# One column of softmax weights brought into row 0 of the masked weights by two transfers through DRAM instead of a ninth transposition

## The chip, the core and the metric

The kernel runs on one core of a Trainium2 chip. The time is that of the whole program on the device, in microseconds (us): the median of several runs. A core has a matrix engine (PE, whose weight loads are listed apart as PEld), a vector engine (DVE), a scalar engine (ACT), a general engine (POOL), and a sequencer (SP) that issues the DMA transfers here. Each of them works through its own instructions strictly in the order in which the program lists them and waits for the others through semaphores. Operands lie in SBUF (128 partitions); PE writes to PSUM, which has 8 banks here; the inputs, the output and some intermediate tiles lie in DRAM. A DMA is issued by SP and is carried by 16 DMA engines, as packets.

## The reference

The input x is (2, 4096, 256). First comes one recurrent attention stage (an RWKV scan with a group norm and an output projection, added to x), then a layer norm and two layers of local attention and a gated feed-forward part. Everything is float32. The change lies in the local attention, which has 8 heads of 64, in windows of 128 tokens that see their own window and the one behind:

```python
bq = q.reshape(b, h, w, WINDOW, d) * QK_SCALE
bk, bv = (look_around(bk), look_around(bv))      # window behind, own window: 256 keys
sim = jnp.einsum('bhwid,bhwjd->bhwij', bq, bk)
i = bt[:, :, None]
j = btk[:, None, :]
mask = (i < j) | (i > j + WINDOW) | (j == -1)
sim = jnp.where(mask, -jnp.finfo(sim.dtype).max, sim)
attn = jax.nn.softmax(sim, axis=-1)
out = jnp.einsum('bhwij,bhwjd->bhwid', attn, bv)
```

Query number i of a window sees its own keys 0 to i, and of the window behind the keys i to 127. That makes 129 keys for each query, and the last key behind, number 127, is seen by every query.

## The kernel before

**Steps.** The two layers of both sequences are 32 blocks of 512 tokens; each block has four windows, so the attention is 128 steps n, one window each. Four of them are the first window of a sequence in a layer ("lone": no window behind). The other 124 steps do what is told here. The first 64 steps are the two layers of the first sequence. Its recurrence comes before them; that of the second sequence runs as filler between the first 55 steps or so, and the feed-forward matmuls of an earlier block fill the rest of each step (`fill`).

**129 columns in place of 256.** `scores` (line 1086) makes, for a pair of heads, a bank of 256 columns: the keys behind, then the own keys. `softmax` (line 1110) takes the columns from 127 on: column 0 is the last key behind, columns 1 to 128 are the own keys. Where an own key k is after the query, and so masked, `copy_predicated` first writes the score of key k-1 behind into its place, since just those are visible. So tile `pr` (128 queries x 8 heads x 129) holds all the visible weights without a gap; ACT makes the exponentials, and ACT or DVE scales each head by its reciprocal sum (the groups `pr<-pr,sums`, ACT line 520 and DVE line 518). Column 0 is also added to column 1 beforehand.

**Two products.** `values` (line 1183) computes the output of a step, transposed, as own values times all 128 weights, plus a correction: `dv` holds, in row k, value k-1 behind minus own value k (row 0: value 127 behind minus own value 0), and `pB` holds the same weights where they belong to a key behind, zero elsewhere, with row 0 the weights of the last key behind. `pB` is 128 keys x 8 heads x 128 queries.

**`transpose_p`** (line 1157) is called twice per step, for four heads each time (s = 0 and 1). PE transposes the four 128x128 blocks of `pr` into a bank; ACT or DVE copies the bank to `pT`, and DVE multiplies it by the mask `backs` into `pB`. With s = 1 comes the part that the change replaces: the 8 columns number 0 (128 queries x 8 heads) are transposed by PE into 8 rows of a bank, copied to the tile `last` by ACT or DVE, and sent by one DMA from these 8 partitions to row 0 of `pB`. `pB` has one buffer, `last` two, `pr` two.

**Where `pB` is needed.** The matmuls of `values(n)` stand in one piece with `scores(n + 1)`, behind the 16 matmuls of the scores; the correction matmuls (`bank<-pB,dv`) read all rows of `pB`, row 0 too.

**What sets the order.** The kernel does not issue its instructions directly. `Plan.note` records each operation with its reads and writes; `Plan.cost` (line 302) gives it a duration; `Plan.order` (line 376) then plays the engines forward. Each engine takes next the operation that can start first, and among those the one with the earlier due row (`plan.at(n)`). Consecutive matmuls into one bank are a piece and stay together. Copies marked `either` go to ACT, or to DVE when ACT is busy for more than 700 ns longer. `Plan.give` (line 508) writes the result down; that is why nearly every instruction carries its line, 524 (`scaled` on ACT: 520, on DVE: 518). A DMA is entered with a landing time and the time that it occupies the queue:

```python
o.passes = size / 170 if ways == 16 else size / (25 * ways)
inner = len(views) == 2 and not any(v.place.outer for v in views)
o.step = 370 if not inner else 580 if ways in (1, 16) else 800
o.time = LAND + o.passes
```

with `LAND = 2500` (ns). All DMAs are issued by SP, in one planned order. Between the steps' other work SP issues, for each step, `vr<-vt` (three DMAs: the values behind moved down by a row, read by POOL for `dv`), `h<-x` (four: the shift before the feed-forward part), a table `tab`, the row of `pB`, and in every second step `kT<-kT`.

Of the kernel before, what the change touches and what calls it, by code (L numbers as in the profile page):

```python
# [9 lines left out]
F32 = mybir.dt.float32  # L10
# [5 lines left out]
P = 128  # L16
B, S, D = 2, 4096, 256
HD_A = 16
L, HEADS, DH, W = 2, 8, 64, 128
# [41 lines left out]
LEAN = 700  # L61
SLACK = 1.06
LOAD = 1283
LAND = 2500
TURN = {"row": 195, "col": 95, "full": 199}
SETS = {AF.Exp: 1, AF.Tanh: 1, AF.Gelu: 2, AF.Ln: 3}
# [15 lines left out]
class View:  # L82
# [51 lines left out]
    def to_broadcast(self, shape):  # L134
        return View(
            self.place,
            self.rows,
            np.broadcast_to(self.idx, shape[1:]),
            [*self.chain, ("to_broadcast", (shape,), {})],
        )  # L140

    def bitcast(self, dtype):
        return View(self.place, self.rows, self.idx, [*self.chain, ("bitcast", (dtype,), {})])
# [37 lines left out]
class Plan:  # L181
# [35 lines left out]
    def bank(self, shape):  # L217

        return self.view(Place(T, True), 0, shape)

    def dram(self, shape, name):
        place = Place(int(np.prod(shape[1:])))
        place.outer = True
        place.real = self.dram_pool.tile([P, place.size], F32, tag=name, name=name)
        return self.view(place, 0, shape)

    def at(self, row):
# [74 lines left out]
    def cost(self, o):  # L302

        views = [*o.outs, *o.ins]
# [4 lines left out]
        if o.eng == "tensor":  # L309
            trans = name == "transpose"  # L310
            left = o.args[1]
            move = o.args[2] if len(o.args) > 2 else o.args[1]
            cols = max(move.idx.size, left.idx.size) if not trans else P
            o.step = (1 if trans else 2) * (cols / 1.2 + (2 if cols >= 256 else 3))
            if not trans and left.shape[0] <= 64:
                o.half = "row"
            elif not trans and left.idx.size <= 64:
                o.half = "col"
            if o.half != "full":
                o.step /= 2  # L320
            o.time = o.step + 150
        elif o.eng == "vector":
            d = 150 + 1.04 * n
            if name == "tensor_tensor_reduce":
                d = 240 + 1.04 * n
            elif name == "tensor_tensor_scan":
                d, o.lock = 203 + 2.1 * n, True
            elif name == "scalar_tensor_tensor":
                d, o.lock = 200 + 1.05 * n, inside > 1
            elif name == "tensor_tensor":  # L330
                o.lock = inside > 1
            elif name == "tensor_scalar":
                d, o.lock = 155 + (1.27 if psum else 0.98) * n, not psum and n > 16
            elif name == "tensor_copy" and not psum:
                d, o.lock = 230 + 0.45 * n, n > 16
            elif name == "bn_aggr":
                d = 172
            elif name == "reciprocal":
                d = 147 + 4 * n
            o.step, o.time = max(d - 85, 60), d  # L340
        elif o.eng in ("scalar", "either"):
            d = (160 if psum else 195) + 0.83 * n
            if name == "scaled":
                d = 305 + 0.76 * n
            elif name == "activation":
                o.set = SETS.get(o.args[2])
                if o.args[2] == AF.Identity:
                    d = 365 + 0.87 * n
                elif isinstance(o.kw.get("bias"), View):
                    d += 85  # L350
            o.step, o.time = d - 100, d
            if "accum_out" in o.kw:
                o.time = d + 200
        elif o.eng == "gpsimd":
            o.lock = name != "memset"
            if name == "tensor_tensor":
                d = 430 + 156 * n if ALU.pow in o.args else 140 + 2.22 * n
            elif name == "tensor_scalar":
                d = 230 + 1.12 * n
            else:  # L360
                d = (100 if name == "memset" else 187) + 0.98 * n
            o.step, o.time = d, d
            hold = d if n > 64 else 100
        else:
            v = min(views, key=lambda v: v.shape[0] * v.idx.size)
            size = 4 * v.shape[0] * v.idx.size
            rows = max(v.shape[0] if v.shape[0] > 1 else v.shape[1] for v in views)
            ways = max(k for k in range(1, 17) if rows % k == 0)
            o.passes = size / 170 if ways == 16 else size / (25 * ways)
            inner = len(views) == 2 and not any(v.place.outer for v in views)  # L370
            o.step = 370 if not inner else 580 if ways in (1, 16) else 800
            o.time = LAND + o.passes
# [155 lines left out]
def kernel(ctx: ExitStack, tc: tile.TileContext, a: dict, out: bass.AP):  # L528
# [581 lines left out]
    def softmax(n, g):  # L1110
# [42 lines left out]
        for m in range(2):  # L1153
            ph = prs[n][:, h0 + 2 * m, off:]
            nc.either.scaled(ph, ph, sums[:, m : m + 1])

    def transpose_p(n, s):


# [14 lines left out]
            ALU.mult,  # L1174
        )
        if s:
            pt = bank([P, W])
            nc.tensor.transpose(pt[:HEADS, :], pr[:, :, 0], ident)
            last = tile_of([P, W], "last", 2)[:HEADS]
            either(last, pt[:HEADS, :])  # L1180
            nc.sync.dma_start(out=pBs[n][0:1], in_=last)

    def values(n):

# [187 lines left out]
    for b, parts in enumerate(ARENA):  # L1372
        o = 0
# [231 lines left out]
```

## Time and profile before

| | |
|---|---|
| median of 3 runs | 2972.16 us (2969.49 to 2972.76) |
| the profiled execution, its own time | 2970.99 us |
| its span (first to last instruction) | 2969.2 us |
| PE busy | 2945.0 us, 99% |
| weight loads (PEld) | 1913.7 us, 64% |
| DVE, ACT, POOL busy | 76%, 68%, 49% |
| DMA engines | 20.9% on the queue of SP's transfers |
| TensorE clock granted | 0.998 |
| transpositions of the four-head blocks, `mats,pr 128*128` | 1024 |
| transpositions of column 0, `mats,pr 128*8` | 124, 33.8 us busy |
| copies of them to `last` | 97 on ACT (24.2 us), 27 on DVE (7.3 us) |
| DMA issues `pB<-last` | 124, 0.69 us each on SP |

In rows of groups the name before `<-` is the tile that is written, behind it those that are read; `128*8 128x128` means weights of 128x8 and 128 columns streamed. A matmul's listed duration holds its way through the pipeline, so matmuls overlap: how long one holds PE up is read from the distance between starts. An `[idle before <-X]` behind a row of the timeline tells how long the engine was idle before it and whose work ended that. For SP the timeline lists the time that it spends on issuing a DMA, not the transfer itself. The trace also has every DMA packet with its size, start and duration, and the updates of the semaphores, from which the landing of a transfer follows.

### The profile page before, as it was taken

The page shows a single profiled execution, that of the slowest core. Times are in us where ns is not written, and L with a number is a line of the kernel's source. Part 1 is how long each engine was busy: PE and PEld are TensorE (multiplying, and loading weights), DVE is VectorE, ACT ScalarE, POOL GpSimd, SP SyncE. Part 2 cuts the span into 40 slices and gives each one's busy share as a digit, 9 for nine tenths or more (in the row PEclk, how much of TensorE's full clock was granted, in tenths as well). Part 3 has the DMA queues.
Part 4 walks back from the last instruction along what each step waited for, and adds up shares of the span by engine and source line. Part 5 has one row for each costly group of instructions (what it writes and reads, how often), then busy time and mean ns, then how long its engine had stood idle before and what let it go on. Part 6 is the DMA issues. An engine that isn't in the chain of part 4 may idle for free.

```text
span 2969.2 us, 48964 instructions
## 1 busy us (share of the span) xinstructions
PE 2945.0 (99%) x15548; PEld 1913.7 (64%) x15548; DVE 2250.9 (76%) x5088; ACT 2018.8 (68%) x5359; POOL 1449.3 (49%) x1705
## 2 busy tenths in 40 slices
PE   9999999999999999999999999999999999999998
PEld 4476766666666666666666666666666666666665
DVE  7889999998866788786777677777676676767673
ACT  7887787778666777776666666666666666666663
POOL 2226654555554555445555444545454554555550
PEclk9999999999999999999999999999999999999999
DMA  2324322221121211111122221111112211111110
GB/s 85 114 78 133 115 69 87 75 82 53 60 65 54 83 48 53 56 59 55 52 77 79 74 68 48 61 58 61 55 44 70 70 57 49 58 55 54 47 40 27
DMA packets 185227, 195.09 MB, mean 66 GB/s; under 512 B 27812, under 2 KB 148484, under 8 KB 184456
## 3 DMA queue, kind: packets, MB, share of 16 engines
q1 hardware_dynamic: 184968, 191.96, 20.9%
q8 instruction: 123, 2.02, 0.3%
q14 instruction: 136, 1.11, 0.1%
HBM read 85.46 MB, written 39.85 MB: 42 GB/s over the span
## 4 chain that ended last, share of the span: by engine, by line
PE 92%; DVE 3%; ACT 3%; issue 1%; POOL 0%; DMA 0%; SPq 0%; POOLq 0%; ACTq 0%; DVEq 0%
PE bank L524 92%; ACT pr L524 1%; ACT L524 1%; DVE arena L524 1%; DVE bank L524 0%; ACT pr L520 0%; DVE sq L524 0%; DVE qk L524 0%; DVE h L524 0%; DVE nmx L524 0%; DVE hm L524 0%; DVE pB L524 0%; ACT arena L524 0%; ACT oT L524 0%; ACT hm L524 0%
## 5 line engine op out<-in xcount | busy, mean ns | idle before, releaser
L524 PE MATMUL bank<-wqkv,xT 128*128 128x512 f32 x1536 | 723.8, 596 | 0.5 <-ACT xT L524 0.5
L524 PE MATMUL bank<-hT,w 128*128 128x512 f32 (+1 forms) x1408 | 652.2, 595 | 0.0
L524 POOL TENSOR_TENSOR t<-qk,tab 128x256 f32<-128x256 f32 x512 | 383.6, 768 | 471.2 <-ACT qk L524 362.3
L524 ACT ACTIVATE pr<-bank,nmx 128x129 f32<-128x129 f32 (+1 forms) x1024 | 369.5, 379 | 147.8 <-DVE nmx L524 146.4
L524 PEld LDWEIGHTS bank<-hT,w 128*128 128x128 f32 (+1 forms) x1408 | 254.8, 189 | 260.9 <-issue 247.3
L524 PEld LDWEIGHTS bank<-wqkv,xT 128*128 128x128 f32 x1536 | 266.4, 191 | 210.9 <-issue 207.3
L524 POOL TENSOR_TENSOR rn<-rn,mhalf 128x16 f32<-128x16 f32 x128 | 391.7, 3060 | 8.8
L520 ACT ACTIVATE pr<-pr,sums 128x129 f32<-128x129 f32 (+1 forms) x948 | 334.1, 418 | 40.7 <-DVE pr L524 39.9
L524 DVE COPY_PREDICATED bank<-packs,bank 128x254 f32<-128x254 int32 x496 | 186.4, 420 | 229.8 <-PE bank L524 229.7
L524 PE MATMUL bank<-w,hm 128*128 128x256 f32 x1280 | 294.0, 381 | 0.0
L524 POOL TENSOR_TENSOR dv<-vr,vt 128x512 f32<-128x512 f32 x124 | 165.4, 1334 | 201.2 <-PE bank L524 188.1
L524 PEld LDWEIGHTS bank<-w,hm 128*128 128x128 f32 x1280 | 239.7, 190 | 35.0 <-issue 4.2
L524 ACT COPY qk<-bank 128x512 f32<-128x512 f32 x225 | 132.3, 588 | 170.5 <-PE bank L524 164.0
L524 PE MATMUL bank<-kT,qT 64*128 64x256 f32 (+1 forms) x2048 | 246.1, 380 | 0.4 <-ACT kT L524 0.4
L524 PE MATMUL bank<-wo,oT 128*128 128x256 f32 x1024 | 243.0, 380 | 1.4 <-ACT oT L524 1.3
L524 PEld LDWEIGHTS bank<-wo,oT 128*128 128x128 f32 x1024 | 193.4, 190 | 70.5 <-ACT oT L524 22.6
L524 PEld LDWEIGHTS bank<-kT,qT 64*128 64x128 f32 x2048 | 190.4, 187 | 68.8 <-issue 36.0
L524 DVE TENSOR_TENSOR pB<-bank,backs 128x512 f32<-128x512 f32 x248 | 170.0, 686 | 83.5 <-PE bank L524 56.7
L524 ACT ACTIVATION_READ_ACCUMULATOR pr<-bank,nmx 128x1 f32 x1024 | 221.8, 217 | 0.0
L524 ACT COPY hm<-bank 128x512 f32<-128x512 f32 x170 | 99.8, 587 | 174.1 <-PE bank L524 173.1
L524 PEld LDWEIGHTS bank<-mats,pr 128*128 128x128 f32 x1148 | 134.9, 135 | 115.7 <-issue 73.2
L524 PE MATMUL bank<-pT,vt 128*64 128x128 f32 x2048 | 203.3, 279 | 0.0
(159 smaller groups left out, 5625.3 us busy)
## 6 DMA issues: line engine op xcount, KB each, us to landing
vr<-vt SPq DMA_DIRECT2D x124, 224.0 KB
tab<-in_c_rot_dram SPq DMA_DIRECT2D x128, 128.0 KB
kT<-kT SPq DMA_DIRECT2D x64, 256.0 KB
z<-zd SPq DMA_DIRECT2D x16, 512.0 KB
x<-in_x_dram SPq DMA_DIRECT2D x16, 512.0 KB
x1d<-x SPq DMA_DIRECT2D x16, 512.0 KB
x<-x1d SPq DMA_DIRECT2D x16, 512.0 KB
h<-x SPq DMA_DIRECT2D x128, 64.0 KB
```

What stands on the lines that cost most here:

```text
L520: self.nc.scalar.activation(dst, src, AF.Copy, scale=scale)
L524: getattr(getattr(self.nc, o.eng), name)(*args, **kw)
```

## The change

In the second call of `transpose_p` of each of the 124 steps the transposition, its bank, the copy and the DMA from `last` go. In their place SP issues two DMAs. The first reads column 0 of the 8 heads from `pr` (128 partitions, 8 values of 4 bytes in each, 516 bytes apart) and writes each value to its place in a row of 1024 in a DRAM tile `front` (two of these, used in turn): value of query q and head h to place 128 h + q. The second copies that row of 4 KB to row 0 of `pB`. In the built program the first is a transfer of 128x8x1 and the second one of 1x1024; the second waits for the landing of the first. The planner is told a duration for it: where neighbours in a view aren't one element apart, the queue is taken to be occupied for `SINGLES`, 1500 ns. The whole program is planned anew with these costs.

```diff
+SINGLES = 1500
 LAND = 2500
...
+    def seen(self, pattern, **sizes):
+
+        return View(self.place, self.rows, self.idx, [*self.chain, ("rearrange", (pattern,), sizes)])
...
-        place.real = self.dram_pool.tile([P, place.size], F32, tag=name, name=name)
+        place.real = self.dram_pool.tile([shape[0], place.size], F32, tag=name, name=name)
...
             o.passes = size / 170 if ways == 16 else size / (25 * ways)
+            if any(v.idx.size > 1 and v.idx.ravel()[1] != v.idx.ravel()[0] + 1 for v in views):
+                o.passes = SINGLES
...
+    fronts = [plan.dram([1, HEADS * W], f"front_{i}") for i in range(2)]
+
     def transpose_p(n, s):
...
         if s:
-            pt = bank([P, W])
-            nc.tensor.transpose(pt[:HEADS, :], pr[:, :, 0], ident)
-            last = tile_of([P, W], "last", 2)[:HEADS]
-            either(last, pt[:HEADS, :])
-            nc.sync.dma_start(out=pBs[n][0:1], in_=last)
+            row = fronts[n % 2]
+            nc.sync.dma_start(out=row.seen("o (h q) -> (o q) h", h=HEADS), in_=pr[:, :, 0])
+            nc.sync.dma_start(out=pBs[n][0:1].rearrange("o h q -> o (h q)"), in_=row)
```

## The prediction

> **What bounds the kernel now.** I read the page first, then the chain of waits over a long stretch, then one step in the timeline. The page's busy shares and its chain:
>
> ```profile
> span 2969.2 us, 48964 instructions
> ...
> PE 2945.0 (99%) x15548; PEld 1913.7 (64%) x15548; DVE 2250.9 (76%) x5088; ACT 2018.8 (68%) x5359; POOL 1449.3 (49%) x1705
> ...
> PE 92%; DVE 3%; ACT 3%; issue 1%; POOL 0%; DMA 0%; SPq 0%; POOLq 0%; ACTq 0%; DVEq 0%
> ```
>
> A busy PE need not be PE at its pace, so the chain between 1515 and 2177 us (columns: start, duration, what):
>
> ```profile
> 1 pieces in order of time: start us, us, what
> 1514.98 662.03 PE bank L524 x3611
> ```
>
> For 662 us, some 31 steps, one matmul follows the other and nothing else is on the chain. In the records of the matmuls a 128x512 matmul starts 429 ns after its like, 128x256 after 216, a 128x128 transposition after 109, nearly everywhere. The sum over the span leaves 24.2 us with PE idle (2969.2 - 2945.0). So PE's own work sets the time; what is taken from PE is won, what is added elsewhere is free as long as PE doesn't wait for it.
>
> The step around 1510 us (start, duration, instruction):
>
> ```profile
> 1506.89 0.60 PE L524 MATMUL bank<-mats,pr 128*128 128x128 f32 x4
> ...
> 1508.33 1.46 SPq L524 DMA_DIRECT2D vr<-vt  x2
> ...
> 1508.42 0.69 ACT L520 ACTIVATE pr<-pr,sums 128x129 f32<-128x129 f32 x2 [0.31 <-DVE pr L524]
> ...
> 1509.83 0.83 SPq L524 DMA_DIRECT2D h<-x  x1
> ...
> 1510.76 0.71 PE L524 MATMUL bank<-mats,pr 128*128 128x128 f32 x5
> ...
> 1511.88 0.25 ACT L524 COPY last<-bank 8x128 f32<-8x128 f32 x1
> ...
> 1512.69 0.68 DVE L524 TENSOR_TENSOR pB<-bank,backs 128x512 f32<-128x512 f32 x1
> ...
> 1513.46 0.73 SPq L524 DMA_DIRECT2D pB<-last  x1
> ...
> 1522.07 0.39 PE L524 MATMUL bank<-pB,dv 128*64 128x128 f32 x4
> ```
>
> The weights are complete at 1509.1, the row goes out only at 1513.46, when DVE's masking has ended (row 0 is written by both), and the first reader of pB runs at 1522.07. I took these times for all 124 steps. Counted from the complete weights, masking ends after 1.7 to 13.4 us (median 4.7); pB's first reader starts after 5.8 at the least (the last step), under 8 in 4 steps, under 9 in 13, median 13.1. The old DMA's semaphore is full 1.81 us after its issue starts; from there 1.6 to 10.2 us pass until the reader, median 5.2.
>
> **What is removed.** 124 transpositions. The five of 1510.76 take 0.71 us where the four of 1506.89 take 0.60; in the records the instruction after the eight-column one starts 109 ns later (median): 124 x 0.109 = 13.5 us, on the path, as PE is saturated. Its weight load (87 ns) lies beside the matmul before. The copies (97 on ACT, 24.2 us, and 27 on DVE, 7.3 us) lie beside PE on engines busy for 68 and 76%: nothing. One bank less is in use for about 1 us a step: between nothing and the 8.1 us that weight loads wait for DVE's work in banks (they run beside matmuls): nothing.
>
> **What is added, and its cover.** (a) SP issues one DMA more per step: 0.33 (128x1024, SBUF to DRAM) to 0.70 us (kT, 4x128 pieces); I take 0.7 for the shape with several dimensions: 124 x 0.7 = 87 us on a queue whose 1544 issues last 915 us together. Hidden. (b) The column transfer, from issue to landing; call it F. It moves 1024 pieces of 4 bytes, 64 per DMA engine, and no such piece to DRAM is in this trace. The nearest row is kT's transfer, alone in this window of 3.04 us:
>
> ```profile
> DMA packets 544, 0.27 MB, mean 88 GB/s; under 512 B 24, under 2 KB 544, under 8 KB 544
> ...
> q1 hardware_dynamic: 544, 0.27, 31.0%
> ```
>
> 0.310 x 16 x 3.04 us / 544 = 27.7 ns a packet; it lands 2.7 us after issue, against 1.8 for the 8 pieces of the old row: 32 packets per engine cost 0.9 us, back to back. Lowest end: 9 ns, the duration of the 4-byte semaphore writes, F = 1.75 + 64 x 0.009 = 2.3. Highest: 189 ns, the mean of the 4 KB packets, F = 13.8. Between: 53.7 ns, the mean over all packets of the queue (20.9% x 16 x 2969.2 / 184968), F = 5.1. I take kT's 27.7, as it too is many small pieces: F = 1.75 + 1.77 = 3.5. (c) The second transfer lands as the table's does (128 KB out of DRAM, 2.05 us after issue), 0.24 later than the old row.
>
> The new row lands at max(0.7 + F, end of masking) + 0.06 + 2.05, counted from the complete weights (0.7: one issue ahead in the queue; 0.06 the wait's end). With F = 3.5 masking still decides in 80 of 124 steps; against each step's reader, one step is late, the last one, by 0.5 us. With 2.3 none is, with 5.1 two by 2.5 us together. The order of the built program keeps that room: PE work between the second group of pr's transpositions and the first pB matmul, at the paces above, is 8.9 us in the median step in both, 5.5 in the least.
>
> (d) SP waits for the column's landing before it issues the row; behind it stand the next `vr<-vt`, `h<-x`, `tab`, `kT<-kT`. In the 80 steps it waited as long for masking. In the others up to 2.5 us are new (0.7 + 3.5 - 1.7). vr serves dv, which POOL writes after the values of the step before and PE reads a step later; h serves POOL and DVE, which already wait for it; tab is loaded a step or more ahead. Nothing on PE; if the cover went, 0.5 us in the 44 steps would be 22 us. (e) The DMA engines get 124 x 1024 x 27.7 ns / 16 = 220 us more, 7% of the span on a queue at 20.9%. (f) All is planned anew. PE has 124 transpositions less and otherwise the same work; ACT loads its tables 111 times instead of 110 (1.28 us each, beside PE). Bounds: at best all PE idle time, 24.2 us, at worst as much again; I take nothing.
>
> Sum against the profiled execution: 2970.99 - 13.5 + 0.5 = 2958.0. That execution is 1.2 us below the median of 2972.16, so the median should be 2959.2, 0.44% less.
>
> **A rule that speaks against it.** kT's row says that cutting a transfer into 512 pieces costs it 0.9 us. [...]
>
> **The rivals.**
>
> *Slow pieces (slower).* If the engines need much longer for 4 bytes into DRAM than for 512 into SBUF, the row is late and PE waits in front of pB's first matmul. For: 16 engines write neighbouring 4-byte places of the same 4 KB, which no row shows. Against: the shortest packets in the trace, 4 bytes (9 ns) and 32 bytes (7 ns), are the quickest. Price by the same maximum over the 124 steps: F = 6.5 (74 ns a piece) makes 19 steps late by 14.0 us in all; that is where it eats the gain. F = 7.0: 23.6 us, so 2982. F = 8.4 (105 ns, the mean of 2 KB packets): 60 us, so 3019. F = 13.8: 475 us, so 3434.
>
> *The queue (same to slower).* SP's order is planned with 4.0 us for the column and 2.5 for the row. Where several issues stand between the two (up to ten in the built order, some waiting for DVE's x), or the column stands behind a vr that waits for POOL, the row goes out later than the maximum says. For: SP's longest wait by sum is POOL's dv, 654.6 us. Against: the masking already held the row back by 4.7 us in the median. At 1.4 us ahead of the column instead of 0.7, F = 5.1 costs some 6 us; the result would be some 2965. If h or vr then drag POOL and DVE too, 22 us as under (d): 2981.
>
> *The transfer is hidden but PE isn't the bound there (same).* The chain's 8% off PE, 240 us, lie mostly before 250 us and around ACT's table loads. If none of the 124 removals in such places counts, 8% of 13.5 go, 1.1 us: 2960. It can't bring the change to nothing.
>
> **How the numbers follow.** What a measurement of this kernel can tell from no change is about 0.2%, 5.9 us. Forecast (hidden, 2954 to 2964): 0.70. Slow pieces with F up to 7: 0.08, half within 0.2%, half slower. Slow pieces beyond 7: 0.09, slower. The queue: 0.13, of which 0.02 still faster by over 0.2%, 0.07 within, 0.04 slower. Faster 0.72, same 0.11, slower 0.17. The range starts at 2954 (5 us of PE's idle time won as well) and reaches to F = 7, 2982; that leaves out the slow pieces beyond 7 and the ends of the plan's bounds, somewhat over 1 in 10. The likeliest case alone: 2954 to 2964.
>
> **What the changed profile would show.** Right: 124 `mats,pr 128*8` rows gone, PE's busy time down by about 13, the chain still one PE piece for hundreds of us, and no wait of PE or PEld on a DMA `pB<-front`. The column's packets: 126,976 of 4 bytes, 64 per engine and step within some 1.8 us, first in the last 4 us before the row goes out. Wrong: rows "PE <- DMA pB<-front" of more than 10 us, packets of 75 ns or more, or SP rows in which the issues after the column are late and POOL's or DVE's idle time on h or vr has grown.

## The result and the profile after

The changed kernel takes 3551.90 us in the median (3546.63 to 3562.96, six runs), against 2971.09 (2969.49 to 2972.76, six runs) for the kernel before. The ratio is 1.196, with a 95% interval of 1.1948 to 1.1972: it is 580.8 us slower, where 13 us less were forecast, in a range that ended at 2982.

The page of the changed kernel (busy time of each engine, share of the span, instructions; then the queue of SP's transfers with packets, MB and share of 16 engines), and below it, from the view of the cores, the granted TensorE clock of the whole run:

```profile
span 3560.0 us, 48615 instructions
...
PE 3118.7 (88%) x15424; PEld 2011.0 (56%) x15424; DVE 2239.7 (63%) x5061; ACT 2011.1 (56%) x5263; POOL 1423.7 (40%) x1705
...
q1 hardware_dynamic: 312192, 192.48, 24.2%
```

```profile
core 0: 3560.0 us, clock 0.944
```

PE has its 124 transpositions less (15548 to 15424) and yet is busy 173.7 us longer, and it is idle for 3560.0 - 3118.7 = 441.3 us, where it was idle for 24.2. So the 590.8 us between the two spans are 417.1 of new PE idle time and 173.7 of longer PE work. The granted clock of the whole run is 0.944 after and 0.998 before: the remaining PE work (2945.0 - 13.5 = 2931.5 us) at that clock would take, as an estimate, 2931.5 x 0.998 / 0.944 = 3099 of the 3118.7 us, so most of the longer work goes with the lower clock.

Cut into stretches, it is seen where this begins. Of the kernel before, and then of the changed one (columns: stretch, its length, busy time and instructions of PE, PEld, DVE, ACT and POOL, then the granted clock, the DMA engines' share and GB/s):

```profile
0.00:250.00 250.00, 239.42 (x780) 137.26 (x780) 204.84 (x418) 194.35 (x343) 76.15 (x144) 1.00 0.30 101
250.00:1000.00 750.00, 746.16 (x4093) 496.04 (x4093) 646.57 (x1461) 556.73 (x1487) 402.21 (x480) 1.00 0.25 76
```

```profile
0.00:250.00 250.00, 239.76 (x779) 137.29 (x779) 205.03 (x418) 194.09 (x341) 75.87 (x144) 1.00 0.30 101
250.00:1000.00 750.00, 639.47 (x3283) 425.09 (x3282) 537.55 (x1207) 454.86 (x1188) 326.08 (x397) 0.93 0.31 63
1000.00:2000.00 1000.00, 877.53 (x4446) 570.84 (x4447) 619.23 (x1416) 569.74 (x1531) 417.41 (x479) 0.94 0.23 51
2000.00:2900.00 900.00, 800.82 (x4130) 517.94 (x4130) 543.94 (x1253) 472.96 (x1314) 366.74 (x429) 0.95 0.25 52
```

The first 250 us, before the first column transfer (issued at 271.2), are the same. From there on PE is idle for 11 to 15% of every stretch, and just there the clock falls from 1.00 to 0.93 to 0.95.

The waits of the changed kernel (engine and line, what it waited for: us in total, times, longest us):

```profile
DVE st L531 <- DMA h<-x: 468.3, 75, 9.7
POOL x L531 <- DMA h<-x: 408.2, 45, 15.6
...
POOL tab L531 <- DMA tab<-in_c_rot_dram: 329.5, 62, 13.3
...
PE bank L531 <- DMA pB<-front: 166.6, 64, 6.8
```

The last row is the wait that the prediction named as the sign of its failure. It explains 166.6 of the 441.3 us of PE's idle time. The three above it were much smaller before, when their line was 524:

```profile
POOL x L524 <- DMA h<-x: 141.8, 41, 11.9
...
DVE st L524 <- DMA h<-x: 30.8, 27, 2.6
...
POOL tab L524 <- DMA tab<-in_c_rot_dram: 21.4, 21, 2.5
```

So h and the table, transfers that the change doesn't touch, have become late.

One step in the timeline of the changed kernel shows how (start, duration, instruction; in brackets the idle time before it and whose work ended it):

```profile
2910.51 0.48 SPq L531 DMA_DIRECT2D front<-pr  x1
...
2911.05 0.86 SPq L531 DMA_DIRECT2D h<-x  x1
...
2913.21 0.51 SPq L531 DMA_DIRECT2D tab<-in_c_rot_dram  x1
...
2914.89 0.69 DVE L531 TENSOR_TENSOR pB<-bank,backs 128x512 f32<-128x512 f32 x1 [0.43 <-ACT pT L531]
...
2921.57 0.24 SPq L531 DMA_DIRECT2D pB<-front  x1
2921.71 0.43 DVE L531 BATCH_NORM_STATS2 st<-h 128x6 f32<-128x256 f32 x1 [6.12 <-DMA h<-x]
2921.75 0.72 POOL L531 TENSOR_TENSOR x<-x,x 128x256 f32<-128x256 f32 x1 [9.06 <-DMA h<-x]
...
2923.71 0.73 POOL L531 TENSOR_TENSOR tab<-tab,qks 128x256 f32<-128x256 f32 x1 [1.24 <-DMA tab<-in_c_rot_dram]
2923.90 0.44 PE L531 MATMUL bank<-pB,dv 128*64 128x128 f32 x4 [2.72 <-DMA pB<-front]
```

The masking of `pB` ends at 2915.58, but the row goes out only at 2921.57, 11.06 us after the issue of the column. By the updates of the semaphores the column lands at 2921.49. h, issued 0.54 us behind the column, lands at 2921.68, 10.6 us after its own issue; the table, issued 2.7 us behind, at 2923.58, 10.4 us after its own. Neither is there before the column.

The updates of the semaphores give every landing, counted from the issue on SP. The column lands after 8.87 us at the least, 10.83 in the median and 11.66 at the ninetieth percentile; the second transfer, issued when all is quiet again, after 1.96; the old row from `last` took 1.81. The packets tell another story. The column's 4-byte packets are 7.2 ns long in the mean of a median column, and in 110 of the 124 columns all 1024 are carried by 1.9 us after the issue, in the latest by 3.2. In the column issued at 1884.98 they are carried by 1.7 us, and the 16 updates of its semaphore come only 8.46 to 10.13 us after the issue. What is slow is not the carriage but the completion, which has no row in the packets. And what is issued behind the column shares it. In the step above, h's 15 packets of 512 bytes are carried between 2912.54 and 2912.69, and h lands 9 us later. (With the table it is not the completion alone: of the 384 packets of 1024 bytes that start between 2912.98 and 2921.04, its own and those of two `out_dram<-x`, the median takes 46 ns and the longest 5.29 us.) Landing of all transfers of the changed kernel by how long after the last column they were issued:

| issued after the column | median landing after their own issue |
|---|---|
| 0 to 1 us | 10.63 us |
| 1 to 2 us | 10.09 us |
| 2 to 3 us | 9.67 us |
| 3 to 4 us | 8.89 us |
| 4 to 5 us | 7.99 us |
| 9 to 10 us | 3.43 us |
| 14 us and more | 1.97 us |

The two columns of the table add up to some 11 to 13 us down to the row of 9 to 10. Against its own column, of the 453 transfers that were issued between a column and its landing, 447 land no earlier than the column does, and the other six at most 0.71 us earlier.

The DMA engines' time shows the same from the other side. SP's queue had 20.9% x 16 x 2969.2 = 9929 us of packets and has 24.2% x 16 x 3560.0 = 13785. Of the 3856 more, 1057 are those of 4-byte packets (1265 against 208, by the packets' records); the rest is longer packets of others, such as the 53,888 of 1024 bytes, which took 82 ns in the mean instead of 51.

Pieces of the chain that ended last, near the end of the run; before, one PE piece stood for 662 us on that chain (start, duration, what):

```profile
3466.83 10.60 DMA h<-x
...
3494.73 10.62 DMA front<-pr
3505.42 1.87 DMA pB<-front
...
3507.43 10.84 PE bank L531 x60
```

### The profile page after: what moved, and what is told of

The parts are those of the page before. It is cut to its first block, busy times and chain, and to the rows that moved or that the text cites. A ratio compares the mean times of both kernels' runs of the same rounds, so it can differ in the third digit from the quotient of the medians.

```text
span 3560.0 us, 48615 instructions
## 1 busy us (share of the span) xinstructions
PE 3118.7 (88%) x15424; PEld 2011.0 (56%) x15424; DVE 2239.7 (63%) x5061; ACT 2011.1 (56%) x5263; POOL 1423.7 (40%) x1705
## 3 DMA queue, kind: packets, MB, share of 16 engines
q1 hardware_dynamic: 312192, 192.48, 24.2%
## 5 line engine op out<-in xcount | busy, mean ns | idle before, releaser
L531 PE MATMUL bank<-wqkv,xT 128*128 128x512 f32 x1536 | 744.4, 611 | 0.5 <-ACT xT L531 0.5
L531 DVE BATCH_NORM_STATS2 st<-h 128x6 f32<-128x256 f32 x128 | 54.4, 425 | 612.3 <-DMA h<-x 468.3
L531 PE MATMUL bank<-pB,dv 128*64 128x128 f32 x1984 | 244.5, 322 | 211.8 <-DMA pB<-front 166.6
L531 PE MATMUL bank<-kT,qT 64*128 64x256 f32 (+1 forms) x2048 | 275.0, 406 | 86.4 <-ACT qT L531 64.3
L531 PE MATMUL bank<-wo,oT 128*128 128x256 f32 x1024 | 258.5, 397 | 54.3 <-ACT oT L531 49.4
L531 PEld LDWEIGHTS bank<-pB,dv 128*64 128x64 f32 x1984 | 159.8, 165 | 229.1 <-POOL rs L531 92.5
L531 POOL TENSOR_TENSOR tab<-tab,qks 128x256 f32<-128x256 f32 x128 | 119.7, 936 | 353.5 <-DMA tab<-in_c_rot_dram 329.5
L531 PE MATMUL bank<-pT,vt 128*64 128x128 f32 x2048 | 244.5, 317 | 7.8 <-DVE hm L531 6.3
L531 POOL TENSOR_TENSOR x<-x,x 128x256 f32<-128x256 f32 x64 | 48.1, 751 | 491.5 <-DMA h<-x 408.2
L531 ACT COPY pT<-bank 128x512 f32<-128x512 f32 x195 | 115.2, 591 | 216.8 <-DVE pB L531 127.0
```

Source lines behind the costliest of these rows:

```text
L531: getattr(getattr(self.nc, o.eng), name)(*args, **kw)
```

## The experiments

The theory after these readings: 4-byte writes to neighbouring places in DRAM complete late (10.83 us in the median), the transfers issued between such a column and its landing (h, the table, vr) land no earlier than it does (447 of 453), and through those DVE, POOL and in the end PE are late. The rivals: the row alone, waited for by PE (as the prediction's "slow pieces" had it); the pause of SP before the second transfer; the mere number of small pieces (1024, in whatever memory); and the new plan. Each diff below is against the changed kernel.

### What the removal alone is worth, and the plan: e_none

```diff
-            row = fronts[n % 2]
-            nc.sync.dma_start(out=row.seen("o (h q) -> (o q) h", h=HEADS), in_=pr[:, :, 0])
-            nc.sync.dma_start(out=pBs[n][0:1].rearrange("o h q -> o (h q)"), in_=row)
+            pass
```

> The changed kernel without the two transfers: no transposition of column 0, no DMA to row 0 of pB. Left out of the computation: the weights of the last key behind in the correction (row 0 of pB stays as the mask leaves it). It measures what the removed transposition is worth by itself. Theory D (the column transfer to DRAM is complete only some 10 us after issue, and the DMAs issued behind it with it): the loss is all in the transfers, so PE work less 13.5 us shows in full: 2955 to 2962 us. Rival P (the new plan puts the engines in a worse order, whatever the transfer takes): stays above 3000. Rival W (only the wait of the row, and so of pB's reader, costs): 2955 to 2962 as well.

Measured: 2955.24 us, ratio 0.9944 (0.9928 to 0.9961) to the kernel before, a gain of 16.7 us. Its page:

```profile
span 2953.1 us, 48058 instructions
...
PE 2928.7 (99%) x15424; PEld 1899.5 (64%) x15424; DVE 2227.2 (75%) x5059; ACT 2012.7 (68%) x5265; POOL 1461.0 (49%) x1705
```

PE is busy 16.3 us less and idle for 24.4 us, as before. The removal of the transpositions is worth what the prediction said and a little more, and a plan made anew costs nothing by itself. The granted clock is 1.000, so this is the remaining PE work as measured at full clock; at the changed kernel's 0.944 it would take 2928.7 / 0.944 = 3102 us, near the estimate of 3099. All of the loss, 3551.90 - 2955.24 = 597 us, comes from the two transfers.

### Which of the two transfers: e_colonly and e_nowait

`e_colonly` leaves the second transfer out:

```diff
             nc.sync.dma_start(out=row.seen("o (h q) -> (o q) h", h=HEADS), in_=pr[:, :, 0])
-            nc.sync.dma_start(out=pBs[n][0:1].rearrange("o h q -> o (h q)"), in_=row)
```

> The changed kernel with the column transfer only: no row is sent to pB and nothing reads the DRAM row. Left out of the computation: row 0 of pB. Nothing can wait for the column except the issue of a later DMA on its semaphore. If the loss is the reader of pB waiting for the row: 2955 to 2965 us, as with neither transfer (2955.2). If it is that the transfers issued behind the column land late with it: most of the loss stays, 3300 to 3700 us, with DVE and POOL waiting 250 us or more each for h and tab, and PE waiting for none of the transfers of pB.

Measured: 3523.94 us, ratio 1.1866 (1.1838 to 1.1894). The column lands after 10.56 us. Nothing reads it, nobody waits for its landing to go on with `pB` (SP waits for columns 77.6 us in all, where it was 848.0), and the kernel is 552.7 us slower than before all the same; the row adds only 28 to that. Its waits, all engines first and then PE's own:

```profile
DVE st L531 <- DMA h<-x: 493.8, 85, 9.4
...
POOL x L531 <- DMA h<-x: 382.5, 43, 15.1
...
POOL tab L531 <- DMA tab<-in_c_rot_dram: 253.0, 58, 10.8
```

```profile
PE bank L531 <- ACT oT L531: 159.9, 61, 7.4
PE bank L531 <- DVE qk L531: 71.6, 20, 8.3
PE bank L531 <- ACT qT L531: 54.6, 22, 5.1
```

PE's long waits are for no transfer here. It waits for ACT and DVE, and DVE and POOL wait for h and the table. How the one leads to the other is seen in a piece of the chain that ended last (start, duration, what):

```profile
3441.43 10.13 DMA h<-x
...
3451.68 0.44 DVE st L531
...
3452.24 1.29 DVE qk L531
3453.58 12.08 PE bank L531 x72
```

PE has to wait for DVE, which has to go through its statistics of h first, and these wait 10 us for h. PE is idle for 3522.3 - 3106.5 = 415.8 us, about as long as in the changed kernel, and the clock is 0.946. PE's wait for the row is therefore not what makes the kernel slow: with the row gone, as much idle time stands before other instructions.

`e_nowait` keeps the column and lets the row come from a place in DRAM that is filled once, so that SP doesn't pause for the column:

```diff
+    still = plan.dram([1, HEADS * W], "still")
+    nc.sync.dma_start(out=still, in_=a["x"][0:1, 0:4, :].rearrange("o r d -> o (r d)"))
...
-            nc.sync.dma_start(out=pBs[n][0:1].rearrange("o h q -> o (h q)"), in_=row)
+            nc.sync.dma_start(out=pBs[n][0:1].rearrange("o h q -> o (h q)"), in_=still)
```

> The column transfer is issued as in the changed kernel, but the row of pB is read from another DRAM row that was written once at the start, so neither SP nor the row waits for the column. Left out of the computation: row 0 of pB gets fixed numbers instead of the weights. Theory D: h<-x, vr<-vt and tab that are issued within 9 us behind the column still land late, so DVE still waits some hundreds of us for h and POOL for h and tab; 3100 to 3400 us. Rival W: only the wait of the row costs, so all comes back: 2955 to 2970. Rival P: above 3400, nearly unchanged.

Measured: 3709.04 us, ratio 1.2476 (1.245 to 1.2502). I had expected at most 3400; without SP's pause it is 157 us slower than the changed kernel, not faster. Over 3400 is what the rival of the new plan had been given; `e_none` above, and `e_sb` and `e_pad` below, are planned anew too and lose nothing, so the plan is excluded by them. The greatest of its waits for a transfer:

```profile
DVE st L531 <- DMA h<-x: 553.8, 78, 11.2
```

The column lands after 11.86 us, and the row from the fixed place, 4 KB that don't wait for the column, lands 6.72 us after its issue in the median instead of 1.96. SP's pause (848.0 us in the changed kernel) is thus not what makes the kernel slow. With it fewer transfers are caught: 453 are issued between a column and its landing in the changed kernel, 607 here. The row here isn't ordered behind the column by any wait of the program, and is late too. That is the step that the prediction's (d) did not have.

### The pieces or their destination: e_sb and e_sbn

The same 1024 pieces of 4 bytes, written into SBUF. In `e_sb` the eight of a query go 64 bytes apart into its partition, in `e_sbn` side by side; a transfer of 8 partitions, as with the old `last`, then fills row 0 with what it finds there:

```diff
+    scrs = [tile_of([P, W], f"scr_{i}") for i in range(2)]
...
+            scr = scrs[n % 2]
+            nc.sync.dma_start(out=scr.rearrange("p (h z) -> p h z", h=HEADS)[:, :, 0], in_=pr[:, :, 0])
+            nc.sync.dma_start(out=pBs[n][0:1], in_=scr[0:HEADS])
```

```diff
...
+            nc.sync.dma_start(out=scr[:, :HEADS], in_=pr[:, :, 0])
...
```

> The same 1024 pieces of 4 bytes, 64 per DMA engine, but into a tile in SBUF (128 partitions, 8 places each, 64 bytes apart) instead of DRAM; then the row of pB from 8 partitions of that tile. Left out of the computation: the values don't come to their places in row 0. Only the target memory of the pieces differs, and the second transfer starts from SBUF. Theory D (completion of small writes in DRAM): the column lands 2.3 to 3.6 us after its issue, and the time is 2955 to 2965 us. Rival N (the number of small pieces costs, wherever they go): landing stays near 10.8 us and the time near 3550. Rival P: stays above 3400.

> The 1024 pieces of 4 bytes into SBUF again, but the 8 places of a partition are neighbours (32 bytes in a row) instead of 64 bytes apart. Left out of the computation: the values don't come to their places in row 0. The runs so far: into SBUF 64 bytes apart 2.34 us to land; into one partition of SBUF, all neighbours, 7.2 us; into DRAM 64, 16 and 4 bytes apart 2.8, 3.3 and 10.8 us. If neighbouring small writes wait for one another in SBUF too, eight to a place cost above 2.9 us. If the 7.2 us came from all engines writing to one partition (or from gathering out of DRAM): 2.3 to 2.5 us. The time is 2956 to 2964 either way.

Measured: 2959.98 us, ratio 0.9959 (0.9945 to 0.9974), and 2959.23 us, ratio 0.9959 (0.9944 to 0.9975). The column lands after 2.34 us in both. What SP waited for, in the changed kernel and then in `e_sb`:

```profile
SPq L531 <- DMA front<-pr: 848.0, 115, 10.6
```

```profile
SPq L531 <- DMA scr<-pr: 19.2, 19, 2.3
```

So 1024 pieces of 4 bytes out of `pr` cost little, and the number of pieces is excluded as the cause. In SBUF it also doesn't matter whether they are neighbours: 2.34 us either way. With F = 2.34 the kernel lands within 1 us of the 2959.2 that was forecast for a hidden column.

### Where in DRAM: e_pad, e_rows, e_half, e_qh, e_z4

Five columns into DRAM that differ in what lies next to what. `e_pad` puts the pieces 64 bytes apart and reads any 4 KB back:

```diff
...
-            nc.sync.dma_start(out=row.seen("o (h q) -> (o q) h", h=HEADS), in_=pr[:, :, 0])
-            nc.sync.dma_start(out=pBs[n][0:1].rearrange("o h q -> o (h q)"), in_=row)
+            far = row.seen("o (h q z) -> (o q) h z", h=HEADS, z=16)
+            far.chain.append(("__getitem__", ((slice(None), slice(None), 0),), {}))
+            nc.sync.dma_start(out=far, in_=pr[:, :, 0])
+            nc.sync.dma_start(out=pBs[n][0:1].rearrange("o h q -> o (h q)"), in_=row[:, : HEADS * W])
```

> The changed kernel with the 1024 pieces of 4 bytes 64 bytes apart in DRAM (a row of 64 KB instead of 4 KB, filled once at the start). The second transfer waits for the first as before, and reads the first 4 KB of that row. Left out of the computation: row 0 of pB gets wrong numbers. If the slowness comes from many engines writing into the same few lines of 64 bytes: landing falls to 2.5 to 5 us, the time to 2955 to 3000. If every small write costs its own time wherever it goes in that row: landing near 10.8 us, the time near 3550.

`e_rows` gathers the eight of a query on ACT or DVE first, so that 128 pieces of 32 bytes fill the same 4 KB:

```diff
-            nc.sync.dma_start(out=row.seen("o (h q) -> (o q) h", h=HEADS), in_=pr[:, :, 0])
+            col = tile_of([P, HEADS], "col", 2)
+            either(col, pr[:, :, 0])
+            nc.sync.dma_start(out=row.seen("o (q h) -> (o q) h", h=HEADS), in_=col)
```

> Through DRAM, but with 128 pieces of 32 bytes: ACT or DVE first copies column 0 of the eight heads into a narrow tile (128 x 8), and each query's 8 values go to DRAM as one piece; the 4 KB row comes back to pB in that order. Left out of the computation: the order of row 0 (queries first instead of heads first). Theory D per piece: 1.9 + 128/1024 x 8.9 = 3.0 us to land, hidden, 2957 to 2968 us. Rival L (fixed latency of writes below some size): landing stays at 9 us or more, the time above 3300.

`e_half` sends four heads only, 512 pieces, still 4 bytes apart:

```diff
+            row = fronts[n % 2][:, : 4 * W]
+            nc.sync.dma_start(out=row.seen("o (h q) -> (o q) h", h=4), in_=pr[:, 0:4, 0])
+            nc.sync.dma_start(out=pBs[n][0:1, 0:4].rearrange("o h q -> o (h q)"), in_=row)
```

> The changed kernel with four of the eight heads: 512 pieces of 4 bytes to DRAM, and half a row back to pB. Left out of the computation: heads 4 to 7 of row 0. Theory D as a cost per piece (the writes are completed one after the other somewhere behind the DMA engines, about 8.9 us for 1024): landing 1.9 + 4.5 = 6.4 us after issue; by the table of the prediction at F = 6.4 the pB reader is late by some 10 us in all, and the late h and tab cost more: 2965 to 3100. Rival L (a fixed latency for small writes to DRAM, whatever their number): landing stays at 9 to 11 us, the time above 3400.

`e_qh` puts query q and head h at place 8 q + h, so that eight neighbours come from one partition, not from eight:

```diff
-            nc.sync.dma_start(out=row.seen("o (h q) -> (o q) h", h=HEADS), in_=pr[:, :, 0])
+            nc.sync.dma_start(out=row.seen("o (q h) -> (o q) h", h=HEADS), in_=pr[:, :, 0])
```

> The changed kernel with the DRAM row laid out query by query: place 8 q + h instead of 128 h + q. [...] Left out of the computation: the order of row 0. If any sixteen writes to a line wait for one another: landing near 10.8 us, time near 3550. [...]

`e_z4` puts the pieces 16 bytes apart, with the view of `e_pad` at another step, and gathers the row from these places (`back`, as in `e_gather` below):

```diff
...
+            far = row.seen("o (h q z) -> (o q) h z", h=HEADS, z=4)
...
+            nc.sync.dma_start(out=pBs[n][0:1].rearrange("o h q -> o (h q)"), in_=back)
...
```

> The same with the values 16 bytes apart, four of them in 64 bytes instead of one (spaced run: 2.8 us) or sixteen (changed kernel: 10.8 us). It computes all of the reference. Theory S (writes into one line of 64 bytes wait for one another, about 0.53 us each: 2.3 + 0.53 x the number of writes in a line): landing 4.4 us, time 2956 to 2975. Theory B (a line is larger than 64 bytes, say 256 or more): landing above 8 us, time above 3200. Theory O (only touching neighbours conflict, lines of 16 bytes or less): 2.8 us, the time as with 64 bytes.

Measured, with the kernels above beside them:

| kernel | written | column lands after | median us | ratio |
|---|---|---|---|---|
| changed kernel | DRAM, 1024 x 4 bytes, side by side, neighbours from different partitions | 10.83 | 3551.90 | 1.196 |
| e_half | DRAM, 512 x 4 bytes, the same way | 8.87 | 3230.92 | 1.087 (1.0839 to 1.0902) |
| e_qh | DRAM, 1024 x 4 bytes, side by side, eight neighbours from one partition | 7.54 | 3194.63 | 1.0749 (1.0729 to 1.0768) |
| e_z4 | DRAM, 1024 x 4 bytes, 16 bytes apart | 3.31 | 3072.55 | 1.0338 (1.0315 to 1.0361) |
| e_pad | DRAM, 1024 x 4 bytes, 64 bytes apart | 2.80 | 2968.65 | 0.9989 (0.9978 to 1.0001) |
| e_sb, e_sbn | SBUF, 1024 x 4 bytes, 64 or 4 bytes apart | 2.34 | 2959.98, 2959.23 | 0.9959 |
| e_rows | DRAM, 128 x 32 bytes, side by side | 1.55 | 2965.79 | 0.998 (0.9968 to 0.9991) |

What SP waited for in `e_pad`, and in `e_half`:

```profile
SPq L531 <- DMA front<-pr: 52.3, 45, 2.8
```

```profile
SPq L531 <- DMA front<-pr: 383.3, 110, 6.8
```

Same pieces, same count, same memory: 64 bytes apart instead of 4, the landing falls from 10.83 to 2.80 us and the loss is gone. So it is the nearness of the small writes in DRAM that costs the time. What the runs do not give is a law, and several landings missed what was expected of them. Half the pieces should have landed after 6.4 us if each cost the same, and took 8.87. A line from 2.8 (one piece in 64 bytes) to 10.83 (sixteen) puts four pieces at 4.4, and `e_z4` took 3.31. Neighbours from one partition are slow too, but less so: `e_qh` took 7.54, where 10.8 was expected if any sixteen in 64 bytes wait for one another. `e_rows` was expected at 3.0 and took 1.55. The size of the pieces by itself isn't the price, since pieces of 4 bytes land after 2.34 us in SBUF and after 2.80 in DRAM 64 bytes apart; several of them queueing for one and the same place would fit the table roughly, but is argued, not shown.

`e_pad` and `e_rows` stay behind `e_sb` for reasons that lie elsewhere. `e_pad` fills its larger rows in DRAM once at the start, and PE is busy 235.15 us in the first 250 where it was 239.42; so some 4 of its 8.7 us lie there. For `e_rows`, whose copies go to ACT and DVE, I have not followed its 6 us.

`e_z4`'s time isn't the column's alone: its gathered row lands only after 7.40 us, and PE waits 75.1 us for it. More on this below.

### Can the plan hide it: e_plan

```diff
-SINGLES = 1500
+SINGLES = 8500
```

> The changed kernel with SINGLES = 8500 instead of 1500: the same transfers, but the planner is told 11 us for the column, which is what the trace shows. It computes all of the reference. If the loss is that the planner lets the rows be needed too early, it comes back for the most part: below 3100. If it is that whatever is issued behind the column lands late, the planner (which takes a queue as occupied, so delays the landings of those behind in its own account too) can only put work in between: 3100 to 3400. If neither matters, 3500 or more.

Measured: 3343.55 us, ratio 1.1249 (1.1217 to 1.1282). The column lands after 10.29 us. Told about the duration, the planner wins 208 of the 597 us and no more. PE's wait for the row in this kernel:

```profile
PE bank L531 <- DMA pB<-front: 180.5, 43, 10.9
```

DVE's wait for h is 153.2 us, where it was 468.3: the planner moves other transfers out of the column's way, but the row still comes late for its reader.

### In search of a version that gains: e_gather, e_stage, e_lay

Three other ways to bring the column to row 0. `e_gather` is `e_pad` without the filling at the start and with the row gathered from the places 64 bytes apart, for which the planner is told `SINGLES` too:

```diff
...
+            back = row.seen("o (i z) -> o i z", z=16)
+            back.chain.append(("__getitem__", ((slice(None), slice(None), 0),), {}))
+            nc.sync.dma_start(out=far, in_=pr[:, :, 0])
...
+            nc.sync.dma_start(out=pBs[n][0:1].rearrange("o h q -> o (h q)"), in_=back)
```

> A version that computes all of the reference without the transposition: the 1024 values go to DRAM 64 bytes apart, and the second transfer gathers them from there, 1024 pieces of 4 bytes, into row 0 of pB. Where the spacing alone sets the landing (2.8 us in the run with spaced places): column 2.8 us, row some 2.0 to 3.0 us, hidden behind masking and the reader's distance, no filling of the row at the start: 2955 to 2962 us, faster than before by 0.3 to 0.5%. If gathering small pieces from DRAM is slow as scattering them is: the row lands 5 us or more after its issue, 2980 or more.

Measured: 3050.73 us, ratio 1.028 (1.0264 to 1.0296). The column lands after 2.77 us as in `e_pad`, but the row after 7.24 in the median and 5.74 at the least, although its 1024 packets are carried by 2.0 us after its issue in the median step. PE's wait for it:

```profile
PE bank L534 <- DMA pB<-front: 57.0, 41, 5.8
```

Once more the completion is late and not the carriage, this time for 4-byte pieces written side by side into one SBUF partition. `e_sbn`, with neighbours in SBUF but spread over 128 partitions, did not show it. Whether the one partition or the scattered reading from DRAM does it, no run tells apart.

`e_stage` uses no DRAM. Each half gathers its four columns on ACT or DVE, a transfer brings 16-byte pieces into one partition, and a copy puts them into row 0 of `pB`:

```diff
...
+        col = tile_of([P, 4], "col", 2)
+        either(col, pr[:, 4 * s : 4 * s + 4, 0])
+        line = tile_of([P, 4 * W], "line", 1)[0:1]
+        nc.sync.dma_start(out=line.seen("o (q h) -> o q h", h=4), in_=col)
+        either(pBs[n][0:1, 4 * s : 4 * s + 4], line.seen("o (q h) -> o h q", h=4))
```

> A version without DRAM and without the transposition: for each group of four heads, ACT or DVE copies column 0 into a narrow tile (128 x 4), one DMA puts its 128 pieces of 16 bytes one behind the other into a single partition, and ACT or DVE copies that line, heads first, into row 0 of pB. It computes all of the reference. Theory D: 128 pieces into SBUF land in about 2 us, PE has 13.5 us less to do, ACT and DVE some 1.7 us a step more, which lies beside PE: 2955 to 2966 us, faster than before. Rival N: 128 pieces a transfer, an eighth of the pieces, cost an eighth of 9 us and are hidden: the same. Rival P, or copies that don't fit beside PE: 2975 or more.

Measured: 2968.89 us, ratio 0.9988 (0.9979 to 0.9998). The line lands after 1.92 us. Its page:

```profile
PE 2932.5 (99%) x15424; PEld 1899.5 (64%) x15424; DVE 2254.4 (76%) x5143; ACT 2242.4 (76%) x5680; POOL 1458.1 (49%) x1705
```

PE is busy 12.5 us less, as it should be. But ACT is busy 224 us longer than before, most of it 195 copies at 1.1 us out of the one partition, and PE is idle for 2964.5 - 2932.5 = 32.0 us instead of 24.2. What is left is 0.12%, less than a measurement can well tell from no change; 2955 to 2966 us were expected. Of the three it is the only one that is not slower than the kernel before.

`e_lay` lays `pB` out as key, query, head, so that a query's eight values go to row 0 as one piece of 32 bytes:

```diff
...
-            pBs[n] = tile_of([P, HEADS, W], "pB", PBS)
+            v = raws[n] = tile_of([P, W, HEADS], "pB", PBS)
+            pBs[n] = View(
+                v.place, v.rows, v.idx.transpose(1, 0), [*v.chain, ("rearrange", ("p q h -> p h q",), {})]
+            )
...
+            col = tile_of([P, HEADS], "col", 2)
+            either(col, pr[:, :, 0])
+            nc.sync.dma_start(out=raws[n][0:1], in_=col)
```

> A version that computes all of the reference, without the transposition and without DRAM: pB is laid out key by query by head, so that its row 0 takes 128 pieces of 32 bytes as they come from the queries (column 0 is first copied into a narrow tile of 128 x 8 by ACT or DVE); one DMA of 4 KB, landing in about 2 us. DVE then writes pB with steps of 32 bytes, and PE streams it with steps of 32 bytes. If both do this at the pace of neighbours: 2955 to 2963 us. If PE streams such columns more slowly, the 1984 pB matmuls, 192.6 us busy before, show it, by up to their double: up to 3150.

Measured: 3080.15 us, ratio 1.0364 (1.0348 to 1.0379). The row lands after 1.92 us; the price is elsewhere. The instructions on `pB` (duration in ns: least, median, greatest; first and last start):

```profile
L531 PE MATMUL bank<-pB,dv x1984: 389/402/415, 277.8 to 3028.0; 128*64 128x128 f32 x199
L531 DVE TENSOR_TENSOR pB<-bank,backs x248: 1049/1087/1118, 269.2 to 3021.1; 128x512 f32<-128x512 f32 x124
```

The medians of the changed kernel are 273 and 684 ns. 1984 matmuls that are 129 ns longer could be up to 256 us if each stood alone; they overlap (in the kernel before, 1984 of 273 ns keep PE busy for 192.6 us), and the kernel lost 109. DVE's longer products lie beside PE, which is busy for 99% of the span here; which share of the 109 each row has was not told apart.

## Why the prediction was wrong

**The bound** was right: PE sets the time, and its idle time is what was lost.

**The removed part** was right. 13.5 us were predicted, all on the path; `e_none` won 16.7 and `e_sb`, with both transfers hidden, 12.0.

**(a), SP's issues,** were over-priced and are indeed no matter: the two take 0.485 and 0.242 us on SP in the median where the old row took 0.693, so a step has 0.03 us more of them, not 0.7.

**(b) is the step that failed first.** It priced the column by the durations of packets: "I take kT's 27.7, as it too is many small pieces: F = 1.75 + 1.77 = 3.5". The packets are even shorter than the lowest bound, 7.2 ns against 9, and had F followed from them it would have been 1.75 + 64 x 0.0072 = 2.2, about what the same pieces take into SBUF (`e_sb`, 2.34). Into neighbouring places in DRAM F is 10.83. It lies within the two ends, 2.3 and 13.8, but the value was taken near the wrong one, and the reason that was written against the slow end ("the shortest packets in the trace ... are the quickest") speaks of carriage, which here said nothing of completion.

**(c)** was right: the second transfer lands 1.96 us after its issue, 2.05 were taken.

**(d) is the step that cost the most.** "Nothing on PE; if the cover went, 0.5 us in the 44 steps would be 22 us" counted only the time that SP holds back the issues that stand behind the row. The transfers issued between the column and the row are not held back, and land as late as the column does (447 of 453). `e_colonly`, in which SP has no row to issue and PE no row to wait for, has 553 of the 581 us. Even a column with the right F would have been priced wrongly by this step.

**(e)** came out near its sum for the wrong reason: 220 us per engine were predicted for the column's packets, and 3856 / 16 = 241 us were added, of which 1057 / 16 = 66 are those of 4-byte packets; the rest is the longer packets of others.

**(f), the plan,** was right to be taken at nothing (`e_none`).

**The rival "slow pieces"** had the right sign, a reason near the right one (16 engines writing neighbouring 4-byte places of the same 4 KB; by `e_qh` neighbours from one partition are slow too) and, for the reader's wait, the right price: its maximum over the 124 steps gives 184 us in 80 steps for F = 10.8, and PE waited 166.6 us for `pB<-front` 64 times. That the two come so near is partly luck: the 184 rest on the readers' places in the kernel before, which the late h and tables have moved, and with the row left out altogether (`e_colonly`) only 28 us come back. The price as a whole, 2972 + 184 - 13.5, would be some 3143 us, and 3552 were measured. What it lacked are the late transfers of (d), and the lower clock, at which PE's work takes some 170 us more by the estimate above. Its chance, 0.17 over both parts, was too low for a case that no row of the trace could exclude.

**The rearranged reading** of `pr` isn't the price: with it, `e_sb` (2.34) and `e_pad` (2.80) took 1.3 and 1.5 times the old row's 1.81 us, where the changed kernel's column took 10.83 / 1.81 = 6.0 times.

**The rival "queue"** had the wrong path: without SP's pause (`e_nowait`) the kernel is slower still, and with no row to come late (`e_colonly`) it is nearly as slow. Its sign, h dragging POOL and DVE, did come, but from transfers that land late and not from issues that are held back, and at many times its 22 us. **"PE isn't the bound there"** has nothing for it; `e_none` wins more than the whole sum.

**The signs** that were named did their work: `PE <- DMA pB<-front` of more than 10 us, and idle time of POOL and DVE on h. The sign for slow pieces, packets of 75 ns or more, was the wrong one: the packets stayed at 7.2 ns.

## What to carry to other kernels

Price a transfer by its landing, from issue to the last update of its semaphore, and not by its packets (7.2 ns each here, and a landing after 10.83 us); where the form of its destination is not in the trace, its landing is unknown and that alone deserves a wide range. Of the transfers issued behind a late column 447 of 453 landed no earlier than it did, so ask what stands behind a late transfer in the queue, whether or not the program orders it. Small pieces that must go to DRAM, side by side 10.83 us here, are to be kept apart (64 bytes, 2.80 us here) or joined before they go (32 bytes, 1.55 us here); if they are kept apart, the way back has its own price, 7.24 us where the row was gathered 4 bytes at a time (`e_gather`).

## What the runs showed of the hardware

- 1024 writes of 4 bytes, side by side in 4 KB of DRAM, are carried within 1.9 us in 110 of 124 columns and complete after 10.83 in the median; 64 bytes apart they complete after 2.80, into SBUF over 128 partitions after 2.34. Gathered 4 bytes at a time into one SBUF partition they complete after 7.24.
- Of 453 transfers issued between such a column and its landing, 447 land no earlier than it does; those issued within 1 us behind it take 10.63 us in the median, those issued 14 us and more behind it 1.97.
- In the runs in which PE was idle for longer, its granted clock was lower: 0.998 with PE busy for 99% of the span, 0.98 with 93% (`e_half`), 0.944 with 88% (the changed kernel), 0.93 with 85% (`e_nowait`). The trace of the changed kernel has only two steps of it, 1.0 and 0.5; 0.5 lasts 396 us in all, in 76 stretches, where it was 11 us before. A wait thus cost more than its own length here: as an estimate some 170 us of longer PE work (3099 - 2931.5) beside 417 of idle time. What in the idle time lowers the clock was not tried.
- A matmul of 128 columns whose moving operand steps by 32 bytes takes 402 ns instead of 273, and DVE's 128x512 product written with that step 1087 instead of 684 (`e_lay`).
